# Attention pairs of a four-layer network: the additions to x move into the next pair, taps, sums, squares and norms to other pairs

## The chip, the cores and the metric

The kernel runs on one core of a Trainium2 chip. The metric is the device time of one execution in microseconds (us), the median of several runs; lower is better. The engines are written as the profile writes them: PE (TensorE, matrix products and transposes), DVE (VectorE), ACT (ScalarE), POOL (GpSimd) and SP (SyncE, which here only issues DMAs). Each engine works through its own list of instructions in order.

## The reference, cut to what matters

Four layers on x of shape (4, 256, 64, 64); the first two are the same kind, and the change lies in them:

```python
x = x + L0(gn(x))      # layer 0
x = x + L1(gn(x))      # layer 1
x = x + L2(gn(x))      # a selective scan
x = x + L3(gn(x))      # four smaller selective scans
```

`gn` normalises each of 32 groups of the last axis (columns), over one image, by its mean and variance. L0 and L1 are a gated scan over the image followed by attention over windows of 8x8 pixels:

```python
y   = scan(...)                             # tanh/sigmoid gates, four 1x1 convolutions
q, k, v = split(windows(y) @ qkv_w.T + qkv_b)
idx = top_k(q.mean(2) @ k.mean(2).T, 4)     # four windows for each of 64 windows
out = softmax(q @ k[idx].T) @ v[idx]        # 8 heads of 32 channels
out = image(out) + depthwise3x3(image(v))   # the nine "taps" a channel half
return out @ wo_w.T + wo_b                  # the projection
```

Everything is in float32.

## The kernel before, in words

The four images are worked one after another. For each image there are, in this order: a scan phase of layer 0, a window phase of layer 0, a scan phase and a window phase of layer 1, and then layers 2 and 3. All that the change touches is in the window phases: eight of them, four images by two layers.

The image is cut into eight strips of 8 rows, numbered 0 to 7. A window phase (`window_phase`) takes 64 windows in 32 pairs; pair i belongs to strip `sj = i // 4` and has the place `a = i % 4` in it. The schedule is by hand: what the loop over i emits first runs first on each engine. In one pair, for the two halves h of the heads, it emits:

- `turn(i-1, h)`: PE transposes the weights of the pair before (tile `pt_ps`, L596), which `turned` copies out, one half by DVE and one by ACT (`pts`, L607 and L609).
- `scores`: PE makes the next scores (`sc`, L545); DVE takes their smallest value (`smallest`, `mn`, L557); ACT takes the exponentials with their sums (`exps`, `pr`, L568); DVE takes the reciprocal of the sums (`sm`, L580) and POOL multiplies by it (`normalise`, L583).
- `values(i-1)`: PE multiplies by v (`ov_ps`, L622); DVE adds the result to the strip's image (`own_rows`, L633).

Beside this each pair carries other work. At a = 1 and a = 2, PE projects the strip before (`project`, into `conv_ps`, L232, emitted in the middle of the pair after `scores(i, 1)`), and `add` (L643, DVE) adds the projection to x, in one half of the channels at a = 1 and the other at a = 2. Before the change `add` is emitted near the end of the same pair. At a = 3 (strips 4 and 5) and a = 0 (strips 5 and 6), a `query` convolution is emitted at the same place as the projection, and an ACT instruction (L298) reads it out at the end of the pair. POOL does one step of the taps in each of pairs 0 to 24 (L253, L256; the weighing step and the squares of `gn` share one buffer, tag "sq"), and DVE nine taps (`dve_taps`, L270), in pairs 2 to 10.

The `gn` of the next layer is worked in steps, at the ends of pairs (`ends`) or in their middle, after `scores(i, 1)` and `smallest(i, 1)` (`mids`). In the window phase of layer 0, `gn` prepares strips 0 and 1 for layer 1: sums on DVE (L143), a small matmul of the sums (`gn_pm`, L134), then centre (DVE L149, POOL L151), square (ACT L156), reduce (DVE L160), a second small matmul (`gn_pv`), then scale (DVE L167, POOL L168 and L172). In the window phase of layer 1, `stats` takes mean and variance of strips 0 to 6 for layer 2: sums (L200), `gn_pm` (L195), mean (L206), four ACT squares with sums (L215), `gn_pv`, variance (`gvar`, L221). Steps planned past pair 31 are left for after the loop.

The tile `conv_ps` of the projections and queries and the small tiles `gn_pm` and `gn_pv` have one tag, "mm". The pool of the window phase is opened with `bufs=1`, and this tag asks for no more: there is one such buffer in PSUM, and the next tile in it has to wait until what reads the last one has run. The other PSUM tiles of the phase are `sc` and `pt_ps` (two buffers each) and `ov_ps` (one).

Of the kernel before, what the change touches and what calls it, by code (L numbers as in the profile page):

```python
# [8 lines left out]
F32 = mybir.dt.float32  # L9
BF16 = mybir.dt.bfloat16  # L10
U32 = mybir.dt.uint32
AF = mybir.ActivationFunctionType
# [6 lines left out]
P = 128  # L19
NB = 4  # L20
C = 256
S = 64
# [22 lines left out]
class Net:  # L45
# [33 lines left out]
    def attention_layers(self, x, w_drams, v_drams):  # L79
        tc, nc = self.tc, self.nc  # L80
        with ExitStack() as ctx:
# [3 lines left out]
            norm = ctx.enter_context(tc.tile_pool(name="at_n", bufs=2, reuse_waits="tile"))  # L85
# [103 lines left out]
            def stats(s, psum):  # L189
                xs = x.rearrange("p (c h w) -> p c w h", c=2, w=S)[:, :, strip[s], :]  # L190
                box = {}

                def columns(tag, part):
                    box[tag] = psum().tile([P, NT], F32, tag="mm", name=f"gn_{tag}")
                    nc.tensor.matmul(box[tag][:, 0:4], self.one_gn, part, start=True, stop=True)  # L195

                def sums():
                    box["s1"] = self.small.tile([P, 4], F32, tag="gn_s1", name="gn_s1")
                    xr = x.rearrange("p (n w) -> p n w", w=S)[:, :, strip[s]]
                    nc.vector.tensor_reduce(  # L200
                        box["s1"], xr.rearrange("p n (g t) -> p g n t", t=2), AX.XY, ALU.add
                    )

                def mean():
                    box["mean"] = self.small.tile([P, 4], F32, tag="gn_mean", name="gn_mean")
                    nc.vector.tensor_scalar(  # L206
                        box["mean"], box["pm"][:, 0:4], -1.0, None, ALU.mult
                    )

                def squares():  # L210
                    box["s2"] = self.small.tile([P, 4], F32, tag="gn_s2", name="gn_s2")
                    sq = norm.tile([P, 2, 8, S], F32, tag="xn", name="gn_sq")
                    for g in range(4):
                        two = slice(2 * g, 2 * g + 2)
                        nc.scalar.activation(  # L215
                            sq[:, :, two], xs[:, :, two], AF.Square,
                            bias=box["mean"][:, g : g + 1], accum_out=box["s2"][:, g : g + 1],
                        )

                def variance():  # L220
                    nc.vector.tensor_copy(self.gvar[:, 4 * s : 4 * s + 4], box["pv"][:, 0:4])  # L221

                return (
                    sums, lambda: columns("pm", box["s1"]), mean, squares,
                    lambda: columns("pv", box["s2"]), variance,
                )

# [248 lines left out]
            def window_phase(lay, work, psum, idx, nxt, taps):  # L476
# [77 lines left out]
                def smallest(i, h):  # L554
                    if i < n_pair:
                        mn[h] = self.small.tile([P, 4], F32, tag="mn", name="mn", bufs=4)
                        nc.vector.tensor_reduce(  # L557
                            mn[h], sc[h].rearrange("p r w m n -> p (w m) r n"), AX.XY, ALU.min
                        )
# [101 lines left out]
                dve_taps = lepe(lay, NW - 1)[:9]  # L661
# [3 lines left out]
                def plan(steps, *where):  # L665
                    for f, (at, i) in zip(steps, where):
                        if i < n_pair:
                            at.setdefault(i, []).append(f)
                        else:
                            left.append(f)  # L670

                if nxt:
                    load_scan_weights(nxt)
                    plan(gn(nxt, 0, lambda: psum), (ends, 10), (ends, 11), (mids, 12),
                         (ends, 12), (mids, 13), (ends, 15), (mids, 16))
                    plan(gn(nxt, 1, lambda: psum), (ends, 14), (ends, 16), (mids, 17),
                         (ends, 18), (mids, 19), (ends, 27), (mids, 28))
                else:

                    for s in range(NW - 1):  # L680
                        i = 4 * s + 6
                        last = i + 6 if s < 5 else i + 3
                        plan(stats(s, lambda: psum), (ends, i), (ends, i + 1), (mids, i + 2),
                             (ends, i + 2), (ends, last), (mids, last + 1))
                for i in range(n_pair):
                    sj, a = divmod(i, 4)
                    add = evict = None
                    exps(i, 0, (0, 1))
                    if i:
                        turn(i - 1, 0)  # L690
                        scores(i, 1)
                        turned(0, 0)
                        turned(0, 1)
                        smallest(i, 1)
                    exps(i, 0, (2, 3))
                    for t in mids.get(i, ()):
                        t()
                    if i == 0:
                        for f in early:
                            f()  # L700
                    normalise(i, 0)
                    if a == 3 and sj + 2 in (NW - 2, NW - 1):
                        evict = query(lay, sj + 2, 0, psum)
                    elif a == 0 and sj + 1 in (NW - 2, NW - 1):
                        evict = query(lay, sj + 1, 1, psum)
                    elif a in (1, 2) and sj:
                        add = project(sj - 1, a - 1, psum)
                    exps(i, 1, (0, 1))
                    if i:
                        turn(i - 1, 1)  # L710
                    scores(i + 1, 0)
                    if i:
                        turned(1, 0)
                        turned(1, 1)
                        values(i - 1)
                    smallest(i + 1, 0)
                    exps(i, 1, (2, 3))
                    normalise(i, 1)
                    if i:
                        own_rows(i - 1)  # L720
                    for t in taps[i : i + 1]:
                        t()
                    for t in dve_taps[i - 2 : i - 1] if i > 1 else ():
                        t()
                    if add:
                        add()
                    if evict:
                        evict()
                    gather(i + 3)
                    if a == 0 and 1 < sj + 1 < NW - 2:  # L730
                        double(sj + 1)
                    elif a == 1 and sj + 1 in (NW - 2, NW - 1):
                        double(sj + 1)
                    indices(i + 4)
                    for t in ends.get(i, ()):
                        t()
# [24 lines left out]
            for i, lay in enumerate(layers):  # L761
                with tc.tile_pool(name=f"at_a{i}", bufs=1, reuse_waits="tile") as work, tc.tile_pool(
                    name=f"at_p{i}", bufs=5, space=PSUM, reuse_waits="tile"
                ) as psum:
                    box["psum"] = psum
                    scan_phase(lay, work, psum, tail)
                    idx = routing(lay, work, psum)
                    taps = lepe(lay, NW - 2, psum)[:9]
                    for s in range(2, 5):
                        evicts = [query(lay, s, m, psum, nc.vector) for m in range(2)]  # L770
                        for t in taps[3 * s - 6 : 3 * s - 3]:
                            t()
                        for evict in evicts:
                            evict()
                    later = lepe(lay, NW - 2, pool=True)[17:]
                    for t in later[:9]:
                        t()
                with tc.tile_pool(name=f"at_c{i}", bufs=1, reuse_waits="tile") as work, tc.tile_pool(
                    name=f"at_q{i}", bufs=1, space=PSUM, reuse_waits="tile"
                ) as psum:  # L780
                    nxt = layers[i + 1] if i + 1 < len(layers) else None
                    box, tail, left = window_phase(lay, work, psum, idx, nxt, later[9:])
                    if nxt is None:
                        box["psum"] = psum
                        g = stats(NW - 1, lambda: psum)
                        for t in (left[0], tail[0], left[1], tail[1], g[0], left[2], left[3], *g[1:]):
                            t()


# [1379 lines left out]
```

## Time and profile before

The median of three runs is 12063.5 us (12038.54 to 12067.32). The profiled execution took 12063.26 us; its span from first to last instruction is 12061.5 us, so 1.8 us lie outside it.

| | us |
|---|---|
| Profiled execution: its time / its span | 12063.26 / 12061.5 |
| The eight window phases, first copy of pair 1 to the last copy but one | 2039.5 |
| Layer 0, four images | 253.6, 252.4, 242.7, 254.2 |
| Layer 1, four images | 261.5, 258.8, 261.9, 254.4 |
| Busy in the eight: PE / DVE / ACT / POOL | 1838.9 / 1297.1 / 1304.0 / 1348.1 |
| Layers 2 and 3 of the second image, for size | 2040.1 |

One stretch of this is read pair by pair from the timeline of DVE: from the start of the first L607 copy of pair i to that of pair i + 1, in us, mean over the four images.

| pairs | layer 0 | layer 1 |
|---|---|---|
| 1 to 3 | 7.67 7.63 6.24 | 8.77 6.62 6.24 |
| 4 to 7 | 6.09 8.46 7.79 7.15 | 5.98 8.35 9.15 6.79 |
| 8 to 11 | 7.56 8.35 8.95 6.79 | 7.47 8.89 9.07 6.59 |
| 12 to 15 | 8.87 11.21 9.77 5.66 | 8.99 11.81 8.25 6.18 |
| 16 to 19 | 9.25 13.45 6.91 9.93 | 6.39 9.98 8.43 5.87 |
| 20 to 23 | 7.23 8.08 7.06 5.98 | 9.70 10.41 8.23 6.00 |
| 24 to 27 | 7.02 8.08 6.91 9.37 | 9.28 10.83 8.23 6.88 |
| 28 to 31 | 9.70 11.49 6.91 5.11 | 8.27 12.47 12.83 6.18 |

In the profile, a row of the timeline has the start in us, the duration in us, engine, source line, operation, the tiles written and read, the number of instructions merged into the row and, in brackets, how long the engine had been idle before it and what released it. In a table of windows, each engine has its busy time with the number of instructions behind it, and PEclk is the share of its full clock that PE was granted.

### The profile page before, as it was taken

How to read it: one execution, taken by the hardware profiler on the slowest of the kernel's cores; microseconds unless marked ns; L12 is line 12 of the kernel's file. 1: busy time of each engine (PE TensorE's matmuls, PEld its weight loads, DVE VectorE, ACT ScalarE, POOL GpSimd, SP SyncE). 2: the span in 40 equal slices, each digit the busy share in tenths (PEclk: the TensorE clock that was granted, in tenths of full speed). 3: DMA queues.
4: the chain of work that ended last, by engine and by line, in shares of the span. 5: the costliest groups of instructions: out<-in, count | busy, mean ns of one | idle time of the engine just before them, and what ended most of it. 6: DMA issues, size and time to landing. Idle time of an engine off the chain costs nothing. (4 is left out here: it accounts for less than half of the span.)

```text
span 12061.5 us, 191725 instructions
## 1 busy us (share of the span) xinstructions
PE 10131.8 (84%) x70632; PEld 5859.0 (49%) x71104; DVE 9899.0 (82%) x8422; ACT 7019.9 (58%) x13096; POOL 8706.7 (72%) x5918
## 2 busy tenths in 40 slices
PE   8998887777899788777789988877779998887777
PEld 4564554444456455444445645544444554554444
DVE  7677998998767799899876779989987677998998
ACT  4555555776455555577645555557764555554776
POOL 4555886898455688789845568868984566886897
PEclk9998998999999899899999989989999998998999
DMA  3343454554334355455433435545543343554554
GB/s 97 98 126 127 170 176 146 170 182 161 90 98 125 128 171 176 147 168 182 161 91 100 126 127 174 173 146 169 181 161 93 95 128 129 175 172 148 168 175 154
DMA packets 682506, 1742.09 MB, mean 144 GB/s; under 512 B 88897, under 2 KB 194897, under 8 KB 681313
## 3 DMA queue, kind: packets, MB, share of 16 engines
q1 hardware_dynamic: 676448, 1721.41, 44.2%
q8 instruction: 563, 9.22, 0.3%
q10 hardware_dynamic: 5120, 8.39, 0.3%
q14 instruction: 375, 3.06, 0.1%
HBM read 1601.52 MB, written 94.39 MB: 141 GB/s over the span
## 5 line engine op out<-in xcount | busy, mean ns | idle before, releaser
L1013 POOL TENSOR_TENSOR hc<-h,cb 128x1024 f32<-128x1024 f32 x2056 | 4812.6, 2353 | 787.0 <-DVE h L1007 348.3
L1007 DVE TENSOR_TENSOR_SCAN h<-da,m_state,pb 128x1024 f32<-128x1024 f32 x1248 | 2920.1, 2340 | 162.6 <-DVE pb L1001 3.9
L959 PE MATMUL y<-ident,hc 128*128 128x128 f32 x16384 | 2355.7, 291 | 449.0 <-POOL hc L1013 347.9
L959 PEld LDWEIGHTS y<-ident,hc 128*128 128x128 f32 x16384 | 2053.0, 151 | 1131.5 <-POOL hc L1013 578.3
L1001 DVE TENSOR_TENSOR pb<-du,pb 128x1024 f32<-128x1024 f32 x1672 | 2024.7, 1211 | 134.4 <-PE pb L931 106.0
L943 ACT ACTIVATE da<-delta,m_v 128x1024 f32<-128x1024 f32 x1672 | 1899.0, 1141 | 135.7 <-DVE h L1007 119.4
L931 PE MATMUL pb<-m_parts,pick 128*128 128x512 bf16 x2840 | 971.9, 413 | 837.1 <-DVE h L1007 771.4
L583 POOL TENSOR_SCALAR pr<-pr,sm,zero 128x256 f32<-128x256 f32 x2048 | 1142.9, 575 | 667.2 <-DVE sm L580 666.3
L568 ACT ACTIVATE pr<-sc,mn 128x256 f32<-128x256 f32 x2048 | 954.9, 480 | 520.0 <-DVE sm L580 352.9
L931 PEld LDWEIGHTS <-pick 128*128 128x128 bf16 x3312 | 262.7, 101 | 1784.8 <-DVE h L1007 984.5
L1007 DVE TENSOR_TENSOR_SCAN h<-da,pb 128x1024 f32<-128x1024 f32 x424 | 969.7, 2287 | 55.5 <-DVE pb L1001 0.9
L917 POOL TENSOR_TENSOR bb<-du,bb 128x1024 f32<-128x1024 f32 x376 | 889.4, 2365 | 127.7 <-DMA bb<-m_cd 115.6
L557 DVE TENSOR_REDUCE mn<-sc 128x4 f32<-128x1024 f32 x512 | 628.2, 1228 | 360.2 <-PE sc L545 357.7
L596 PE MATMUL pt_ps<-ident,pr 128*128 128x128 f32 x4096 | 662.3, 304 | 79.5 <-POOL pr L583 33.1
L1007 DVE TENSOR_TENSOR_SCAN h<-dap,m_state,bb 128x1024 f32<-128x1024 f32 x288 | 672.2, 2334 | 69.0 <-ACT dap L943 50.8
L232 PE MATMUL conv_ps<-att_y,att_wb 128*128 128x512 f32 x1536 | 690.1, 599 | 11.3 <-DVE gn_mean L206 11.3
L596 PEld LDWEIGHTS pt_ps<-ident,pr 128*128 128x128 f32 x4096 | 522.7, 157 | 257.3 <-POOL pr L583 106.6
L545 PE MATMUL sc<-kv,q_swap 32*64 32x128 f32 x8192 | 621.4, 294 | 13.9 <-DMA q_swap<-q_late 8.4
L943 ACT ACTIVATE dap<-delta,m_v 128x1024 f32<-128x1024 f32 x376 | 419.7, 1116 | 315.6 <-DVE h L1007 229.2
L545 PE MATMUL sc<-kv,att_y 32*64 32x128 f32 x7168 | 590.6, 292 | 14.6 <-DMA kv<-kv_dram 7.8
L607 DVE COPY pts<-pt_ps 128x512 f32<-128x512 f32 x512 | 353.0, 689 | 293.7 <-PE pt_ps L596 292.8
L270 DVE SCALAR_TENSOR_TENSOR lp<-vimg,att_v,lp 128x512 f32<-128x512 f32 x672 | 507.7, 756 | 31.2 <-DVE lp L270 1.4
(300 smaller groups left out, 18037.9 us busy)
## 6 DMA issues: line engine op xcount, KB each, us to landing
cb<-m_cd SPq DMA_DIRECT2D x2048, 512.0 KB, 4.0
kv<-kv_dram SPq DMA_DIRECT2D x1984, 128.0 KB, 2.7
bb<-m_cd SPq DMA_DIRECT2D x376, 512.0 KB, 5.3
kv_dram<-kst SPq DMA_DIRECT2D x128, 256.0 KB, 3.4
kv_dram<-vn SPq DMA_DIRECT2D x128, 256.0 KB, 4.1
q_swap<-att_y SPq DMA_DIRECT2D x96, 256.0 KB, 4.2
m_pe<-in_pe_dram SPq DMA_DIRECT2D x32, 512.0 KB, 4.2
out_dram<-yo SPq DMA_DIRECT2D x64, 256.0 KB, 2.4
```

Source lines behind the costliest of these rows:

```text
L232: nc.tensor.matmul(ps, w[:, k, w0 + m * P : w0 + (m + 1) * P], src[:, k], start=(k == 0), stop=(k == 1),)
L545: nc.tensor.matmul(sc[h][b * 64 : b * 64 + 64, r, w, m, :], (own(sj, m) if r == b else swap[sj % 2][:, m])[rows, 2 * a + w], kv[i, w][rows ...
L568: nc.scalar.activation(t[:, g].rearrange("p j r t -> p r j t"), sc[h][:, :, g // 2, g % 2, :].rearrange("p r (j t) -> p r j t", j=2), AF.E ...
L583: nc.gpsimd.tensor_scalar(t[:, g], t[:, g], s[:, g : g + 1], self.zero, ALU.mult, ALU.add)
L596: nc.tensor.transpose(pt[h][j][:, g, :], t[:, g, j].rearrange("p r t -> p (r t)"), self.ident,)
L917: nc.gpsimd.tensor_tensor(pb[i], slots[i][0]["du"], pb[i], ALU.mult)
L931: nc.tensor.matmul(pb[i][:, ss], self.pick[:, n : n + 1].to_broadcast([P, P]), blk["parts"][:, ss], start=True, stop=True,)
L943: nc.scalar.activation(da[i], blk["delta"], AF.Exp, scale=blk["a"](n))
L959: nc.tensor.matmul(blk["y"][:, ss], t[:, ss], self.ident, is_transpose=True, start=(n == 0 and ss.start % NT == 0), stop=(n == DS - 1 and ...
L1001: nc.vector.tensor_tensor(pb[i], blk["du"], pb[i], ALU.mult)
L1007: nc.vector.tensor_tensor_scan(h[i][:, ss], da[i][:, ss], pb[i][:, ss], state, ALU.mult, ALU.add)
L1013: nc.gpsimd.tensor_tensor(hc[i][:, ss], h[i][:, ss], cb[i][:, ss], ALU.mult)
```

## The change

`add` is kept over the end of the pair and emitted in the next one, after `smallest(i, 1)`. The DVE taps go to pairs with a = 0 or a = 3, from pair 3 on. The four squares of `stats` become four steps. The steps of `gn` and `stats` are planned anew: for layer 0, strip s begins at the end of pair 7 + 4s; for layer 1 at the end of pair 4s + 7 in place of 4s + 6, with one or two squares in each step. What is left after the loop is re-ordered to fit: the mean of strip 6 now lies between the last two projections.

```diff
@@ stats @@
-                def squares():
-                    box["s2"] = self.small.tile([P, 4], F32, tag="gn_s2", name="gn_s2")
-                    sq = norm.tile([P, 2, 8, S], F32, tag="xn", name="gn_sq")
-                    for g in range(4):
-                        two = slice(2 * g, 2 * g + 2)
-                        nc.scalar.activation(
-                            sq[:, :, two], xs[:, :, two], AF.Square,
...
+                def square(g):
+                    if g == 0:
+                        box["s2"] = self.small.tile([P, 4], F32, tag="gn_s2", name="gn_s2")
+                        box["sq"] = norm.tile([P, 2, 8, S], F32, tag="xn", name="gn_sq")
+                    two = slice(2 * g, 2 * g + 2)
+                    nc.scalar.activation(
+                        box["sq"][:, :, two], xs[:, :, two], AF.Square,
...
-                    sums, lambda: columns("pm", box["s1"]), mean, squares,
+                    sums, lambda: columns("pm", box["s1"]), mean,
+                    *(lambda g=g: square(g) for g in range(4)),
@@ window_phase @@
-                    plan(gn(nxt, 0, lambda: psum), (ends, 10), (ends, 11), (mids, 12),
-                         (ends, 12), (mids, 13), (ends, 15), (mids, 16))
-                    plan(gn(nxt, 1, lambda: psum), (ends, 14), (ends, 16), (mids, 17),
-                         (ends, 18), (mids, 19), (ends, 27), (mids, 28))
+                    for s in range(2):
+                        i = 7 + 4 * s
+                        plan(gn(nxt, s, lambda: psum), (ends, i), (ends, i + 1), (mids, i + 2),
+                             (ends, i + 3), (mids, i + 4), (ends, i + 4), (mids, i + 5))
...
-                        i = 4 * s + 6
-                        last = i + 6 if s < 5 else i + 3
+                        i = 4 * s + 7
                         plan(stats(s, lambda: psum), (ends, i), (ends, i + 1), (mids, i + 2),
-                             (ends, i + 2), (ends, last), (mids, last + 1))
+                             (ends, i + 2), (mids, i + 3), (ends, i + 3), (mids, i + 4),
+                             (ends, i + 4), (mids, i + 5))
+                add = None
                 for i in range(n_pair):
                     sj, a = divmod(i, 4)
-                    add = evict = None
+                    evict = None
...
                         smallest(i, 1)
+                    if add:
+                        add()
+                        add = None
                     exps(i, 0, (2, 3))
...
-                    for t in dve_taps[i - 2 : i - 1] if i > 1 else ():
-                        t()
-                    if add:
-                        add()
+                    if a in (0, 3) and i and dve_taps:
+                        dve_taps.pop(0)()
@@ attention_layers, after the last window phase @@
-                        for t in (left[0], tail[0], left[1], tail[1], g[0], left[2], left[3], *g[1:]):
+                        var, left = left[0], left[1:]
+                        for t in (var, tail[0], left[0], left[1], tail[1], *left[2:6], g[0],
+                                  left[6], left[7], *g[1:]):
                             t()
```

More of the change, by code (lines that the diff above doesn't have):

```diff
@@ L208, in mean @@
                     )
-                def squares():
-                    box["s2"] = self.small.tile([P, 4], F32, tag="gn_s2", name="gn_s2")
-                    sq = norm.tile([P, 2, 8, S], F32, tag="xn", name="gn_sq")
-                    for g in range(4):
-                        two = slice(2 * g, 2 * g + 2)
-                        nc.scalar.activation(
-                            sq[:, :, two], xs[:, :, two], AF.Square,
-                            bias=box["mean"][:, g : g + 1], accum_out=box["s2"][:, g : g + 1],
-                        )
+                def square(g):
[5 more added lines that the diff above has]
+                        box["sq"][:, :, two], xs[:, :, two], AF.Square,
+                        bias=box["mean"][:, g : g + 1], accum_out=box["s2"][:, g : g + 1],
+                    )
                 def variance():
```

## The prediction

> **What bounds the kernel now.** The change lies in the eight window phases, so I read the table of windows first, for a stretch without special steps (pairs 22 to 26 of layer 0) and for two whole phases, and a short stretch of layer 1 at a stall.
>
> ```profile
> core 0: us, PE busy (x) PEld busy (x) DVE busy (x) ACT busy (x) POOL busy (x), PEclk, DMA share, GB/s
> 3428.00:3456.00 28.00, 27.84 (x595) 20.56 (x593) 19.25 (x31) 20.75 (x74) 20.99 (x37) 1.00 0.54 153
> 3966.00:3973.50 7.50, 6.11 (x44) 3.37 (x43) 2.07 (x4) 2.53 (x9) 2.18 (x5) 0.55 0.01 2
> 3256.00:3508.40 252.40, 228.07 (x4516) 170.43 (x4514) 159.66 (x248) 155.66 (x560) 174.00 (x280) 0.89 0.49 140
> 3727.10:3985.90 258.80, 230.12 (x4531) 173.89 (x4530) 164.79 (x258) 170.18 (x606) 163.13 (x276) 0.88 0.47 133
> ```
>
> In the quiet stretch PE is busy 27.84 of 28.00 us at full clock, the others about 20: PE is the bound. Second view, the timeline of PE and of DVE in pair 25 there (a = 1, a projection):
>
> ```profile
> 3447.35 1.09 PE L596 MATMUL pt_ps<-ident,pr 128*128 128x128 f32 x8
> 3449.41 1.98 PE L232 MATMUL conv_ps<-vimg,att_wb 128*128 128x512 f32 x4
> 3451.23 1.03 PE L596 MATMUL pt_ps<-ident,pr 128*128 128x128 f32 x8
> 3453.22 1.10 PE L622 MATMUL ov_ps<-pts,kv 128*32 128x64 f32 x64
> 3454.26 1.09 PE L596 MATMUL pt_ps<-ident,pr 128*128 128x128 f32 x8
> ```
>
> ```profile
> 3449.54 1.23 DVE L557 TENSOR_REDUCE mn<-sc 128x4 f32<-128x1024 f32 x1 [0.81 <-PE sc L545]
> 3450.68 0.17 DVE L580 RECIPROCAL sm<-sm 128x4 f32<-128x4 f32 x1
> 3451.86 0.69 DVE L607 COPY pts<-pt_ps 128x512 f32<-128x512 f32 x1 [1.01 <-PE pt_ps L596]
> ...
> 3454.90 1.37 DVE L643 SCALAR_TENSOR_TENSOR x<-conv_ps,att_v,x 128x512 f32<-128x512 f32 x1
> 3456.12 0.73 DVE L607 COPY pts<-pt_ps 128x512 f32<-128x512 f32 x1
> ```
>
> From transposes to transposes the pair takes 3454.26 - 3447.35 = 6.91 us, of which the projection takes 3451.23 - 3449.41 = 1.82; the other five groups (two `pt_ps`, two `sc`, `ov_ps`) share 5.09. The `add` at the end of the pair makes the next copy late, yet the four-pair sum in the table of pairs is 27.77 us (8.08 + 6.91 + 5.87 + 6.91 in its undisturbed cases) against 4 x 6.91 = 27.64 of PE work: **where every pair has a convolution, `add` at the end costs almost nothing.** Third view, waits on the one "mm" buffer, at pairs 29 and 30 of layer 1:
>
> ```profile
> 3965.41 0.36 PE L195 MATMUL gn_pv<-gn_s,one_gn 128*128 128x4 f32 x2 [2.02 <-DVE x L643]
> 3969.92 3.78 PE L232 MATMUL conv_ps<-vimg,att_wb 128*128 128x512 f32 x4 [1.39 <-DVE gvar L221]
> ```
>
> A PE instruction that wants this buffer stands still until DVE has read the last tile in it, with every later matmul queued behind. And the projection after the stall takes 3.78 us, not 1.98: PEclk was 0.55 there.
>
> **The change part by part.**
>
> 1. *`add` half a pair later.* It is now emitted behind `mn` in the middle of the next pair. The projection of a = 1 thus occupies the buffer until DVE, in pair a = 2, has done copy, `mn` and `add`; but the projection of a = 2 stands on PE right behind the `scores` which `mn` waits for. By the rows: `mn` starts at 3449.54, the next DVE instruction may follow 1.14 later, `add` takes 1.37, and a projection starts 0.05 after it (3456.27 to 3456.32, the next such place): 3452.10. PE was free at 3449.41. **The gap is 2.69 us.** Queued behind it on PE are the second transposes, the next scores and `values`, for which DVE, ACT and POOL all wait. Bounds for one case: 0.05 (the present wait there, if `add` were early enough) to 2.69. I take 2.69, because the stretch has no idle PE time to absorb it. Seven strips, eight phases: 56 x 2.69 = 151 us. The queries at a = 3 (strips 4 and 5) meet the same `add` of a = 2: 16 x 2.69 = 43 us. Together **+194**.
>
> 2. *`add` gone from the pair's end.* In pairs a = 3 without a query (40 of them) the late copy was felt, by about 0.6 us; the `add` in their middle now holds the reciprocal, hence POOL's `normalise`, back by 1.37, of which a pair without convolution has about 0.8 of cover. 0.6 off and 0.6 on: **0** (-24 to +32). The reciprocal in pairs a = 2 is also 1.37 late, but POOL's 2.18 us then end under PE's longer pair.
>
> 3. *Sums and variance of layer 1.* The sums (1.22 us) stood behind `add` at the end of a = 2; the interval there is 8.23 against 6.91 in layer 0, 1.32 us for each of 6 strips and 4 images, 32 in all. At the end of a = 3 they delay pair a = 0, which has some cover: about half returns. **-17** (0 to -32). The mean is now read in the middle of a = 1 and the variance at a = 0; before, the other way round. Each holds the convolution there by 1.41 us, 6 times a phase at the projection and twice at a query, before and after: 0. The `gn_pv` of pair 29 no longer waits 2.02 us: 4 images, **-8**.
>
> 4. *Four squares apart.* They stood in a row on ACT, ahead of the next pair's exponentials. In pairs 20 to 23 of layer 1 the undisturbed sum is 8.86 + 9.56 + 8.23 + 5.88 = 32.53, layer 0 has 27.77; two waits of 1.41 and the 1.32 of the sums leave 0.6 for the squares. 28 of them: **-17**. Lower end: the whole 2.9 us each, -81, if the squares cause more of the disturbed cases. One square of 0.76 fits into ACT's idle time.
>
> 5. *Norms of layer 0.* The steps move to earlier pairs with their prices: `gn_sq` still shares its buffer with the taps and again follows an even pair, where POOL adds a tap (it held ACT for 5.6 us at pair 12); the scale's 1.65 + 1.90 us on POOL leave pair 28 for pair 16. One more mean is read ahead of a projection (pairs 9 and 13, not 17 alone): 4 x 1.41 = **+6**. The DVE taps (0.97 us each) leave four projecting pairs for nine others with some cover: 0 (-9 to +12). No DMA is moved relative to its pair, nor past another on SP's queue.
>
> 6. *After the loop.* `gn_pm` and the mean of strip 6 now lie between the two last projections: about 0.65 us, 4 images, **+3**.
>
> 7. *Cover.* At pair 27 of layer 0, three images wait about 4 us for `q_swap`; a longer pair 26 eats 2.7 of each, and near the stalls of the norms (pairs 10, 14, 18) about half of the gap will be absorbed: **-24**.
>
> 8. *The clock.* [...] a wait of 1.39 us (with some idle time before) stands ahead of the projection of 3.78 us, and in layer 1 the pairs 13, 17, 21, 25, all with a wait of 1.41, come as 9.56 or as 11.26 us (and 13.39 once); 10 of these 16 are the longer ones, by 1.70. [...] 72 gaps of 2.69, two thirds followed by such a stretch: 72 x 0.65 x 1.70 = 80; I take half, **+40**, since some replace stretches that are there now (0 to +120).
>
> Sum: 194 + 0 - 17 - 8 - 17 + 6 + 3 - 24 + 40 = +177 us, added to the profiled execution's 12063.3: **12240 us**. The median of the runs shown is 12063.5, so the base is the same.
>
> **The rivals.**
>
> *Faster: the clock comes back (0.12).* Place: PE in the window phases. PEclk in the eight is 0.85 to 0.91, mean 0.88; 2 x 0.12 x 2039.5 = 490 us at half clock, about half of that lost, 245. Spread squares, sums away from `add`, and norms out of pairs 27 to 29 remove the stalls ahead of many such stretches. Without item 8 the sum is +137; from 137 / 245 = 0.56 of the stretches gone, the kernel is faster; with 0.8 gone, 12063 + 137 - 196 = 12004. For it: the disturbed pairs 12 to 17 and 28 to 30. Against: gaps of 1.4 us precede today's stretches, and the change makes 72 of 2.69.
>
> *No change (0.06).* The gap is met half the time by idle PE time and the gains of items 3 and 4 reach their lower ends: 97 - 32 - 81 + 6 + 3 + 6, about 0: 12063. For it: PE has about 25 us of idle time a phase. Against: little of it lies in pairs a = 2.
>
> *Slower, with the clock in full (0.22).* Item 8 at +120 and cover 0: +281, 12345.
>
> *The change doesn't do what it says.* If the projection did not wait for the old `add`, items 2 to 4 would be left, about 12020. The one buffer speaks against it, and the two rows of pairs 29 and 30; it is in the 0.12.
>
> **How the numbers follow.** The forecast has 0.60 (12150 to 12310), slower with the clock 0.22, no change 0.06, faster 0.12. 0.3% is 36 us, about what a measurement tells from no change. Faster 0.12, same 0.06, slower 0.82. The range leaves out about 1 in 10 on each side: 12040 to 12350.
>
> **What would show it.** Right: before the projection of each a = 2 pair a wait of about 2.7 us for L643, in the totals of waits some 150 us or more of it in place of the present 47 us (81 times); pairs 22 and 26 of layer 0 at about 9.6 us instead of 6.91; PEclk of the phases at or below 0.88; ACT's squares one at a time, without an idle PE behind them. Wrong: no such wait, or a PEclk above 0.93 in the phases.

## The result and the profile after

The changed kernel takes 12234.15 us (median of 4 runs, 12231.3 to 12245.41) against 12058.92 us before (4 runs): a ratio of 1.015, 95% interval 1.0132 to 1.0167. It is slower by 175 us. The profiled execution has a span of 12229.5 us; the eight window phases in it take 2216 us instead of 2039, and everything else 10013 instead of 10022. So the whole loss lies where the change lies.

The profile's view of the tile `conv_ps` says in the part "its engine sat idle before it until" how long PE waited, and for what (us, times; both the weight load and the matmul of a convolution count, so each wait appears twice). First the kernel before:

```profile
  DVE gvar L221: 74.5, 48
...
  DVE x L643: 46.9, 81
```

And the changed kernel, where `add` is L644:

```profile
  DVE x L644: 386.1, 144
  DVE gn_mean L206: 76.1, 56
...
  DVE gvar L221: 29.2, 16
```

144 rows are 72 waits, and 386.1 / 144 = 2.68 us each: 193 us. (The matmuls' rows alone have 2.56 us, those of the weight loads 2.80.) One of them is pair 26 of layer 0 in the second image, here in the timeline of PE and of DVE:

```profile
3526.74 1.09 PE L597 MATMUL pt_ps<-ident,pr 128*128 128x128 f32 x8
3531.43 3.78 PE L233 MATMUL conv_ps<-vimg,att_wb 128*128 128x512 f32 x4 [2.56 <-DVE x L644]
3535.00 1.92 PE L597 MATMUL pt_ps<-ident,pr 128*128 128x128 f32 x8
3539.16 1.09 PE L597 MATMUL pt_ps<-ident,pr 128*128 128x128 f32 x8
```

```profile
3528.93 1.22 DVE L558 TENSOR_REDUCE mn<-sc 128x4 f32<-128x1024 f32 x1 [0.81 <-PE sc L546]
3530.07 1.30 DVE L644 SCALAR_TENSOR_TENSOR x<-conv_ps,att_v,x 128x512 f32<-128x512 f32 x1
3531.27 0.17 DVE L581 RECIPROCAL sm<-sm 128x4 f32<-128x4 f32 x1
```

`mn` must wait for the scores, `add` stands behind `mn`, and the projection behind `add`. Then the projection takes 3.78 us instead of 1.98 and the transposes 1.92 instead of 1.04: after the gap PE runs at half clock (the clock records of the trace have 0.5 from 3530.6 to 3537.4 us). The pair, 6.91 us before, takes 12.42 here and 11.2 in the other images; the prediction had named about 9.6. Of the 72 projections and queries that waited for L644 in this profile, 63 took more than 2.5 us.

The table of windows shows what that does to this pair (first row) and to the two phases shown before (second image, layer 0 and layer 1; PEclk is the last figure but two):

```profile
3527.40:3539.90 12.50, 9.94 (x151) 6.76 (x150) 5.55 (x10) 5.02 (x19) 4.40 (x9) 0.73 0.46 128
...
3294.50:3578.30 283.80, 241.55 (x4514) 178.41 (x4513) 160.52 (x247) 155.83 (x560) 174.07 (x282) 0.83 0.43 125
3798.80:4063.90 265.10, 221.40 (x4531) 161.81 (x4530) 162.66 (x257) 171.08 (x606) 161.69 (x275) 0.92 0.45 130
```

Of the two stalls shown before, the one of `gn_pv` in pair 29 of layer 1 is gone: it runs without a wait, at the end of pair 27. The projection of pair 29 waits for the mean, and that of pair 30 has one of the new waits (timeline of PE, second image):

```profile
4028.20 0.39 PE L195 MATMUL gn_pv<-gn_s,one_gn 128*128 128x4 f32 x2
4038.28 2.94 PE L233 MATMUL conv_ps<-vimg,att_wb 128*128 128x512 f32 x4 [1.42 <-DVE gn_mean L206]
4049.50 3.62 PE L233 MATMUL conv_ps<-vimg,att_wb 128*128 128x512 f32 x4 [2.56 <-DVE x L644]
```

Layer 0 went from 252.4 to 283.8 us at a clock of 0.89 and then 0.83. Layer 1 went from 258.8 to 265.1, but its clock *rose* from 0.88 to 0.92 (in the mean of the four images from 0.87 to 0.90): it gains something and pays for it with the same waits. Over four images layer 0 loses 131 us and layer 1 loses 46.

### The profile page after: what moved, and what is told of

It is laid out like the page before. It is cut to its first block, busy times and chain, and to the rows that moved or that the text cites. A ratio compares the mean times of both kernels' runs of the same rounds, so it can differ in the third digit from the quotient of the medians.

```text
span 12229.5 us, 192213 instructions
## 1 busy us (share of the span) xinstructions
PE 10174.5 (83%) x71104; PEld 5825.5 (48%) x71104; DVE 9892.1 (81%) x8422; ACT 7022.7 (57%) x13096; POOL 8695.0 (71%) x5918
## 5 line engine op out<-in xcount | busy, mean ns | idle before, releaser
L936 PE MATMUL pb<-m_parts,pick 128*128 128x512 bf16 x3312 | 1082.0, 411 | 835.3 <-DVE h L1012 766.2
L233 PE MATMUL conv_ps<-att_y,att_wb 128*128 128x512 f32 x1536 | 720.1, 620 | 54.7 <-DVE x L644 41.0
L597 PE MATMUL pt_ps<-ident,pr 128*128 128x128 f32 x4096 | 660.8, 304 | 64.3 <-POOL pr L584 28.0
L610 ACT ACTIVATE pts<-pt_ps 128x512 f32<-128x512 f32 x512 | 305.2, 596 | 612.4 <-PE pt_ps L597 612.2
L597 PEld LDWEIGHTS pt_ps<-ident,pr 128*128 128x128 f32 x4096 | 524.3, 157 | 269.4 <-POOL pr L584 148.9
L546 PE MATMUL sc<-kv,q_swap 32*64 32x128 f32 x8192 | 596.7, 287 | 2.9 <-DMA kv<-kv_dram 2.9
```

The costliest lines, as they stand in the source:

```text
L233: nc.tensor.matmul(ps, w[:, k, w0 + m * P : w0 + (m + 1) * P], src[:, k], start=(k == 0), stop=(k == 1),)
L546: nc.tensor.matmul(sc[h][b * 64 : b * 64 + 64, r, w, m, :], (own(sj, m) if r == b else swap[sj % 2][:, m])[rows, 2 * a + w], kv[i, w][rows ...
L597: nc.tensor.transpose(pt[h][j][:, g, :], t[:, g, j].rearrange("p r t -> p (r t)"), self.ident,)
L936: nc.tensor.matmul(pb[i][:, ss], self.pick[:, n : n + 1].to_broadcast([P, P]), blk["parts"][:, ss], start=True, stop=True,)
```

## The experiments

Each run is given with its ratio to the kernel before on the same chip. Phase times are means over the four images of one profiled execution for each run, so differences of a few us between them prove little; "half clock" is the time a phase spent at a granted clock of 0.5, added up from the clock records of the trace.

| run | us | ratio, 95% interval | layer 0 phase | half clock | layer 1 phase | half clock |
|---|---|---|---|---|---|---|
| before (first profile) | 12058.9 | 1 | 250.7 | 59.7 | 259.2 | 66.6 |
| the change | 12234.2 | 1.0150 (1.0132 to 1.0167) | 283.4 | 93.8 | 270.7 | 55.3 |
| add_back | 11964.9 | 0.9910 (0.9893 to 0.9928) | 248.0 | 58.7 | 240.9 | 40.1 |
| add_l0 | 12167.8 | 1.0082 (1.0066 to 1.0099) | 272.2 | 64.9 | 265.6 | 87.1 |
| add_early | 11982.6 | 0.9932 (0.9913 to 0.9952) | 247.3 | 46.9 | 241.4 | 27.5 |
| busy_gap | 12105.8 | 1.0037 (1.0024 to 1.0049) | 267.3 | 57.0 | 255.0 | 18.6 |
| stats_only | 11953.8 | 0.9922 (0.9906 to 0.9939) | 245.5 | 49.2 | 234.0 | 20.3 |
| squares_row | 11959.1 | 0.9912 (0.9888 to 0.9936) | 248.7 | 57.8 | 238.3 | 25.0 |
| norms_only | 12054.0 | 0.9995 (0.9987 to 1.0004) | 248.9 | 57.9 | 261.0 | 73.7 |
| taps_only | 12020.9 | 0.9972 (0.9961 to 0.9984) | 246.7 | 54.4 | 252.2 | 52.9 |
| conv_late | 11932.3 | 0.9897 (0.9881 to 0.9914) | 249.8 | 54.1 | 226.1 | 15.0 |
| conv_late_back | 11924.1 | 0.9888 (0.9872 to 0.9905) | 246.6 | 54.6 | 227.8 | 24.7 |
| late_stats | 11949.7 | 0.9913 (0.9888 to 0.9938) | 254.1 | 59.2 | 227.7 | 10.3 |
| conv_late_early | 11924.5 | 0.9896 (0.9878 to 0.9913) | 251.5 | 66.5 | 230.2 | 17.4 |

### Is it the place of `add`?

**add_back.** The changed kernel with `add` again at the end of its pair:

```diff
-                    if add:
-                        add()
-                        add = None
                     exps(i, 0, (2, 3))
...
                         dve_taps.pop(0)()
+                    if add:
+                        add()
+                        add = None
                     if evict:
```

> The changed kernel with one part undone: the addition to x stands again at the end of its own pair; taps, squares, sums and norms stay where the change put them. Theory (the projection waits for the single PSUM buffer until the late addition has read it): the 72 waits of 2.68 us go, 193 us, and with them most of the added half clock, some 45 us; the kernel comes to about 11990 to 12030 us, slightly under the kernel before. Rival (the moved taps, sums, squares and norms cost the time): it stays above 12150 us.

It took 11964.9 us. The waits for `add` are all but gone:

```profile
  DVE x L644: 12.0, 65
```

The late addition thus costs 269 us, more than the whole loss: the rest of the change is worth having. The rival, that the moved taps, sums, squares and norms cost the time by themselves, falls.

**add_l0.** The kernel before, with `add` late in layer 0 alone:

```diff
-                    add = evict = None
+                    evict = None
...
+                    if add:
+                        add()
+                        add = None
                     exps(i, 0, (2, 3))
...
-                    if add:
+                    if add and not nxt:
                         add()
+                        add = None
```

> The kernel before with one part done: in the window phases of layer 0 alone the addition moves into the next pair; all else as before. Theory (the buffer): 9 waits of 2.69 us in each of 4 phases, 97 us, about 40 us of half clock behind them, less 10 to 25 us of cover: about 12059 + 115 = 12175 us, all of it in the layer 0 phases. Rival (layer 0 lost by its moved norms and taps): less than 40 us, under 12100 us.

It took 12167.8 us, 105.6 over the kernel before, near the 115 expected. Not all of it was in layer 0: the layer 0 phases grew by 21.5 us each, 86 in all, and the layer 1 phases, whose instructions are the same as before, by 6.4 each. The last section comes back to that. And the layer 0 phases of the changed kernel, at 283.4 us, are 11.2 longer still. Only the taps and the norms differ there, and each of these, moved alone, leaves layer 0 no longer than before (246.7 and 248.9 us, below). So beside the late `add` they do cost something: more than all of the difference lies in pairs 8 to 15, which take 83.8 us in place of 67.4, with 39.4 us at half clock and not 10.2. In norms_only these pairs take 75.2 us, so the norms are the likelier of the two; it was not tried.

**add_early.** The changed kernel, `add` still in the next pair but ahead of `mn`:

```diff
-                        smallest(i, 1)
-                    if add:
-                        add()
-                        add = None
+                        if add:
+                            add()
+                            add = None
+                        smallest(i, 1)
                     exps(i, 0, (2, 3))
```

> The changed kernel, with the addition still in the next pair but ahead of the smallest value on VectorE instead of behind it. Theory (the buffer): the addition ends about 1.14 us plus the wait for the scores earlier, so the projection waits about 0.6 us and not 2.68; 72 x 2.0 = 145 us and most of the half clock behind the gaps return: about 12030 us. The smallest value is about 0.5 us later in these pairs, at most +35 us. Rival (it is the extra work in the next pair that costs, not its place before the projection): it stays near 12230 us.

It took 11982.6 us, 47 us less than expected. One DVE instruction further up the queue removes 252 us. In the view of `conv_ps`, the wait for `add` (L644) is now:

```profile
  DVE x L644: 96.7, 141
```

That is 0.69 us each in place of 2.68, as the theory had it (0.6).

### Does the gap itself take the clock?

**busy_gap.** The changed kernel with useless work: ahead of each convolution that waits for the late `add`, PE makes the eight transposes of the second half twice, into the tile where they are made again afterwards.

```diff
                     normalise(i, 0)
+                    fill = sj and (a == 2 or a == 3 and sj + 2 in (NW - 2, NW - 1))
+                    if fill:
+                        early_turn(i - 1, 1, 2)
...
                     if i:
-                        turn(i - 1, 1)
+                        turn(i - 1, 1, fill)
```

> The changed kernel with useless work added: ahead of each convolution that waits for the late addition, TensorE makes the transposes of the second half twice more (2.1 us of the 2.69 us gap), and makes them again in their old place; results unchanged. Theory (the gap itself lowers the granted clock): the gaps stay but PE is busy in them, the half clock behind them goes, pairs at a = 2 come to 9.6 us in place of 11.2: 12234 - 60 to -117, about 12120 to 12175 us, faster by more work. Rival [...]: 12234 us or more.

It took 12105.8 us: 128 us *faster* than the changed kernel, by 72 x 16 transposes more. The timeline of PE in the same pair 26 of layer 0, second image (L597 is the useless work, L611 the real transposes):

```profile
3482.10 2.32 PE L597 MATMUL pt_ps<-ident,pr 128*128 128x128 f32 x16
3484.76 1.99 PE L233 MATMUL conv_ps<-vimg,att_wb 128*128 128x512 f32 x4 [0.34 <-DVE x L658]
3486.58 1.04 PE L611 MATMUL pt_ps<-ident,pr 128*128 128x128 f32 x8
```

And that pair, then the two phases, in the table of windows:

```profile
3480.70:3490.30 9.60, 9.13 (x167) 6.87 (x165) 5.54 (x9) 4.98 (x19) 4.36 (x9) 1.00 0.64 167
3259.50:3526.20 266.70, 245.06 (x4658) 186.22 (x4657) 160.34 (x247) 156.02 (x560) 173.34 (x280) 0.88 0.48 133
3744.50:4000.70 256.20, 230.73 (x4676) 174.30 (x4674) 163.04 (x258) 171.31 (x607) 161.83 (x275) 0.96 0.48 134
```

The projection still begins only when `add` is through, but it takes 1.99 us, and the pair takes 9.60 us, which is 6.91 + 2.69. The clock of layer 1 is 0.96. So the price of these waits of PE has two parts, which can be told apart: the wait (193 us in all) and the lower clock after it (3.78 us for the projection and not 1.99). The 128 us that the fill gained are rather too much for the second part. The fill also took away half clock that the late `add` had not made: layer 1 has 18.6 us of it a phase here, and 40.1 in add_back, which has no such gaps. Against add_back the changed kernel has 4 x (35.1 + 15.2) = 201 us more at half clock. The fill removed 294 us of it and shortened the eight phases by 127; at that rate the 201 us cost about 87, which is an estimate.

### What did the other parts bring?

**stats_only.** The kernel before with the layer 1 part of the change (squares as four steps, the new plan, the order after the loop).

> The kernel before with the layer 1 part of the change alone: four steps for the squares, the sums at the end of a = 3, the new plan of mean and variance, and the new order after the loop; addition, taps and layer 0 norms as before. Prediction on record for these terms: -17 for the sums, -17 for the squares, -8 for the second small matmul, +3 after the loop: 12060 - 39 = about 12020 us. If the squares in a row also cause half-clock stretches, as the undone addition suggests (layer 1 phases there 18 us shorter than before), up to -75, about 11985 us. Rival (squares and sums were hidden anyway): 12060 us.

It took 11953.8 us, 103 under the kernel before: beyond the upper case. In the table of windows, the layer 1 phase of the second image:

```profile
3683.60:3921.00 237.40, 215.07 (x4533) 162.18 (x4530) 162.59 (x258) 172.00 (x607) 163.02 (x276) 0.94 0.51 145
```

PE's clock rises from 0.88 to 0.94. Half clock falls from 66.6 us a phase to 20.3.

**squares_row.** The same with the squares in a row again, as four steps at one place:

```diff
-                             (ends, i + 2), (mids, i + 3), (ends, i + 3), (mids, i + 4),
+                             (ends, i + 2), (ends, i + 2), (ends, i + 2), (ends, i + 2),
                              (ends, i + 4), (mids, i + 5))
```

> The run with the layer 1 part alone (11954 us), with one thing undone: the four squares stand in a row again, at the end of the pair with a = 1; sums, mean, variance and the order after the loop as in the change. If the spread squares made the gain (ScalarE held 2.9 us ahead of the next exponentials): back by 50 to 90 us, to 12005 to 12045 us. If the moved sums and the freed buffer at pairs 29 and 30 made it: within 20 us of 11954.

It took 11959.1 us: the ratios of the two overlap. Spreading the squares brings next to nothing; what is left for the gain is the sums, mean, variance and their buffer, which were not tried one by one. In stats_only, with the sums away from `add`, pairs a = 2 of layer 1 take 6.92 us from pair 14 on and not 8.2 to 8.4 (12.8 at pair 30), and pairs 28 to 31 (where `gn_pv` waited behind `add`) take 28.9 us and not 39.7: these four pairs alone give 43 us over four images.

**norms_only** and **taps_only.** The kernel before with the layer 0 plan alone, and with the DVE taps at a = 0 and 3 alone:

```diff
-                    for t in dve_taps[i - 2 : i - 1] if i > 1 else ():
-                        t()
+                    if a in (0, 3) and i and dve_taps:
+                        dve_taps.pop(0)()
```

> The kernel before with the layer 0 norms planned as in the change, nothing else. Prediction on record: +6 us, the same steps at other pairs: 12045 to 12075 us. Rival (pairs 27 to 29, freed of the scale, give back their 10 us a phase): about 12020 us. Second rival (the norms are what made layer 0 slow): over 12100 us.

> The kernel before with VectorE's nine taps at the pairs with a = 0 or 3, nothing else. Prediction on record: -9 to +12, taken as 0. The runs so far leave about +14 for the taps (addition undone 11965, against layer 1 part -103 and norms -3 from 12057, together 11951): expected 12050 to 12080 us. If the taps are free at a = 0 and 3: 12057 or less.

The norms are no measurable difference (0.9995, 0.9987 to 1.0004). The taps gain 32 us (0.9972), where I expected a small loss; that expectation came from adding up parts, and they do not add up. In layer 0 the gain is in pairs 4 to 11 (31.7 to 28.5 us in pairs 8 to 11), where the tap no longer stands ahead of `add`; the waits for `add` in the view of `conv_ps` fall from 46.9 to 25.2. That this is the whole cause is not shown: in the profile the larger part of the gain is in layer 1 (7.0 us a phase against 4.0).

### Can both be had?

**conv_late.** The changed kernel, with the block that emits `project` and `query` moved down:

```diff
                     normalise(i, 0)
-                    if a == 3 and sj + 2 in (NW - 2, NW - 1):
-                        evict = query(lay, sj + 2, 0, psum)
...
                     scores(i + 1, 0)
+                    if a == 3 and sj + 2 in (NW - 2, NW - 1):
+                        evict = query(lay, sj + 2, 0, psum)
...
```

> The changed kernel, its addition still late, but TensorE takes the projections and queries later in the pair: behind the second transposes and the next scores (2.0 us of work) instead of ahead of them. Theory (the wait is for the buffer, and only what stands behind it in TensorE's order suffers): the gap of 2.68 us shrinks to about 0.65, and the waits of 1.41 us for mean and variance vanish behind the same work; under the version with the addition put back (11965 us), about 11880 to 11940 us. Rival (the later projection now delays the values and the next transposes by as much): 12000 us or more.

11932.3 us. PE does the second transposes and the next scores while DVE reads the buffer out; the late `add` then costs little, and the waits for mean and variance shrink with it. In the view of `conv_ps`, the wait for `add` is 0.64 us each:

```profile
  DVE x L644: 81.9, 128
```

**conv_late_back, late_stats, conv_late_early.** The late projections with `add` at the end of its own pair; the same on the kernel before with the layer 1 part only; and with `add` in the next pair ahead of `mn`.

> Both: the addition at the end of its own pair and the projections and queries behind the second transposes and the next scores. Theory: no wait for the buffer at all, about 11870 to 11930 us, and less half clock than in any run so far. Rival: the projection now ends only about 1 us ahead of the addition, which may hold the first copy of the next pair longer: no better than 11965 us.

> A version meant to beat both: the layer 1 part of the change, addition, taps and norms as before, and the projections and queries behind the second transposes and the next scores on TensorE. Theory: the layer 1 phases as in the runs with the late projection (about 227 us), the layer 0 phases at or under 246 us: 11890 to 11925 us. Rival (taps at a = 1 and 2 now stand ahead of an addition whose projection ends late, and hold the next copy): 11940 us or more.

> The changed kernel with the projections late on TensorE and the addition in the next pair but ahead of the smallest value. Theory: the projection's remaining wait of about 0.65 us for the addition goes; pairs at a = 2, from pair 8 on, come from 7.7 to about 7.0 to 7.3 us, but the smallest value is 0.5 us later in pairs a = 3, which have no convolution to cover it: 11900 to 11935 us, level with or just under the versions so far (11924 and 11932). Rival (the addition at the end of its own pair is the better place once nothing waits for the buffer): over 11940 us.

11924.1, 11949.7 and 11924.5 us, in ratios 0.9888, 0.9913 and 0.9896, with intervals that overlap. conv_late_back came in as expected, but not with less half clock than any run so far (conv_late has less). late_stats missed its 11925 and landed on the side of the rival, level with stats_only; its layer 0 phases are the slowest of the three (254.1 us). The rival's reason, the taps at a = 1 and 2, is not borne out: pairs 1 to 11 of layer 0, which hold these taps, take 84.0 us in late_stats and 84.6 in conv_late_back, while pairs 28 to 31, in which the old plan still has steps of the norms, take 34.8 against 28.2. The ratios don't separate the three versions. All of them beat both kernels; conv_late_back is 133 us under the kernel before. In conv_late_early no projection waits for the addition in the pair loop any more, as expected, and pairs a = 2 of layer 1 take 7.15 us from pair 8 on (conv_late: 7.69); its pairs a = 3 are longer by about as much on the way (8.53 against 8.23), so nothing is left of it. A second PSUM buffer for the tag, which might take the wait away, was not tried.

## Why the prediction was right

The forecast was 12240 us, and 12234 was measured. The mechanism named for it is shown: the waits are there in number and length (item 1: 72 of 2.69 us predicted, 72 of 2.68 measured), undoing `add` alone turns the loss into a gain, and the way out goes through PE's order at the one buffer.

The sum fits better than its terms: errors in both directions cancel, and that the total came within 6 us is luck. One of its signs held only in part: PEclk was 0.83 to 0.85 in layer 0, but in layer 1 it came to 0.89 to 0.92, above the 0.88 that was named.

- **Item 8, the clock, was too small.** It took 40 us, half of two thirds of the gaps, since some stretches would only replace others. The estimate above is about 87 us, and busy_gap's 128, just over the stated upper bound of 120, is an upper figure: 63 of 72 gaps were followed by slow convolutions, not two thirds. That these gaps cost clock at all is measured: with PE at work in them (busy_gap) a phase had 57.0 us of half clock in layer 0 and 18.6 in layer 1, in place of 93.8 and 55.3, and the kernel took 128 us less.
- **Items 3 and 4 with the small item after the loop were too small in the other direction.** They took -39; stats_only measured -103. What was left out was again the clock: the working reckoned the pairs that ran undisturbed, 32.53 us against 27.77, and set the longer cases aside, while the moved steps removed most of the half clock (66.6 to 20.3 us a phase). The split was wrong too: the squares, put at -17, brought about 5 us, within the noise; the sums, mean, variance and buffer brought the rest, 43 us of it in pairs 28 to 31, where the text had 8 for the one wait.
- **Item 2** (`add` gone from the end of the pair, against `add` in the middle of a = 3) and **item 7** (cover) can only be seen together: the late `add` costs 269 us, of which 193 are waits and 87 to 128 clock, so 11 to 52 us are cover and relief; the text had 24.
- **Item 5**: the norms at +6 measured -3 with zero inside the interval. The taps at 0 (-9 to +12) measured -32, outside the bounds: what a tap costs ahead of `add` at a = 1 and 2 was sized too small. How much of the 32 is clock was not tried.

The parts measured alone add up to -103 - 3 - 32 + 269 = 131 us, not 175. Of the 44 us between them, 41 lie among the parts without the late `add`: these bring 138 us when measured alone and 97 together, in add_back against the kernel before on its chip. One place is on record: the layer 1 phases of add_back are 6.9 us longer than those of stats_only (28 us over four images), although only the taps differ there. Why the parts don't add is left open. The faster rival had its mechanism right. The clock did come back in layer 1 (half clock 66.6 to 55.3 us, in spite of 36 new gaps), but far from the 0.56 of all stretches that it needed, since layer 0 went from 59.7 to 93.8.

## What to carry to other kernels

Before a reader of a buffer is moved later, look for who writes that buffer next and what that one's queue holds behind it: here, with one buffer, a read that was hidden at the end of a pair became 72 waits of the busiest engine, 2.68 us each, when the next write stood ahead of it. If the reader cannot move, move the next writer behind other work of its own engine; here that came to 11932 us, while two better places for the read came to 11965 and 11983. And price an idle stretch of PE twice, for its length (2.68 us here) and for the slower matmuls after it (3.78 us for a projection in place of 1.98); if the second part is in doubt, fill the gap with useless matmuls and measure.

## What the hardware showed that was not expected

Work that computes nothing made a kernel 128 us faster, 1%: busy_gap took 12105.8 us, the changed kernel 12234.2. No stretch in the clock records of the profiles before and after is shorter than 3.41 us. For a count, the records were cut into steps of this length, and the share of each step in which a matmul ran was set against the clock of the next step. In the profile before, of 199 steps at full clock with PE busy less than 40%, 198 were followed by half clock; between 40% and 75%, 91 of 553; above that, none of 2219. The profile after gives 232 of 232, 97 of 567 and 3 of 2212. Only 28 of the 431 steps under 40% had no matmul at all. So in these two profiles half clock followed 430 of 431 steps with a low busy share, most of them with matmuls in them; between 40% and 75% the share alone does not tell what follows. The two bounds were chosen for the count; what sets the clock is not shown.

The same instructions can also take different times, with more or less half clock. The layer 1 phases of the kernel before, of norms_only and of add_l0 hold the same instructions, and took 259.2, 261.0 and 265.6 us, with 66.6, 73.7 and 87.1 us at half clock; the layer 0 phases of stats_only, unchanged as well, are 5.2 us shorter than before. Each is one execution, and the executions of the kernel before on one chip lie between 12007 and 12085 us, so whether the edit in another phase moved them is not shown. Either way, a difference of some 25 us over four images, in a phase that was not touched, is no sign of a cause there.
